# First edge layer of a two-layer graph network: a ring of 14 gathered tiles per stream, gathers issued tile by tile, one-hots turned one step ahead, a new order of the step

## The chip, the core and the metric

The kernel runs on one core of a Trainium2 chip. The metric is the device time of one execution in microseconds. The core has five engines that run on their own and wait for one another through counters: PE (TensorE, matrix products into PSUM), DVE (VectorE), ACT (ScalarE), POOL (GpSimd, which here issues the indirect loads) and SP (SyncE, which issues the other loads and stores). Each works through its own instructions in the order in which the program gives them.

## The reference, cut to what matters

A graph of N = 6250 nodes with E = 100000 edges, sorted by their destination `dst`; 512 features in 8 heads of 64. Two layers follow one another, each on a normalized input, with a residual. The first, which is changed, is attention over the edges that arrive at a node:

```python
h = leaky_relu(feat @ W.T + b, 0.2).reshape(N, 8, 64)
e_src, e_dst = (h * w_att_src).sum(-1), (h * w_att_dst).sum(-1)
e = leaky_relu(e_src[src] + e_dst[dst], 0.2)
m = segment_max(e, dst);  ex = exp(e - m[dst]);  s = segment_sum(ex, dst)
a = ex / s[dst] * dist
out = segment_sum(h[src] * a[:, :, None], dst)
```

The second layer takes the mean of `x[src]` over the edges of a node, two matrix products and a normalization.

## The kernel before, in words

**Stages.** A prologue normalizes x, multiplies it by the weights and writes `h0_d`: one row of 520 numbers per node, 512 of h and 8 of e_src. Its gathers for the first steps are issued at 242.5 us and after. Then comes the first edge layer (adds from 317.5 to 1575.3 us), a change-over, the second edge layer (adds from 1617.7 to 2802.9 us) and a short end.

**Tiling.** The sorted edges are cut into NQ = 4 streams. Each stream has 196 tiles of 128 edges, and a step k takes T = 3 tiles (j = 0, 1, 2) of each stream, so there are NW = 66 steps, the last of one tile. A gather (L717) is one indirect load of 128 rows of 2080 bytes for one stream and one tile: 12 a step. Its rows land in `gbuf`, which holds NB = 4 steps: 4 x 4 streams x 3 tiles x 520 numbers in each partition. The gathers of step k+4 are put into the program at the end of step k, stream by stream and in a stream tile by tile, into the slots of step k. A gather therefore waits for the adds (A..) of step k that read its slot.

**What a step does.** Streams go in two pairs, p = 0 and p = 1. The names are those of the table `STEPS`; the number ahead of a function there says for which later step the work is done in the pass of step k.

- OH (L760, DVE): one-hot matrices of the 128 edges of each tile against the 64 destination rows of the window. FT0, FT1 (L779, PE) turn them, for p = 0 and 1, in one PSUM bank ("t"); FT0c, FT1c (L783, ACT) copy the result to `oht`.
- FD (L791, PE): e_dst of each edge, as a product with `oht`, into the bank "z", once for each p. EC (L803, ACT) picks the e_src column out of the gathered rows into `es`; SS (L797, PE) adds it in "z", by three products, one per tile.
- EZ (L809, ACT) copies "z" to `e`. NX (L822, DVE) scans the first LA = 2 tiles of it backwards for the running maximum that the step before needs; SCF (L815) scans forwards; SCR (L829) joins both.
- TE, TM (L841, PE) turn `e` and the maxima back to one edge per partition; CM (L846, ACT) copies them; LM, SUB (DVE), EXP (ACT), AA (L871, L875, DVE) give the weights of the edges.
- D0a, D0b, D1a, D1b (L935, DVE), D0c (L942, DVE) and H01 to H13 (L954, ACT) multiply the gathered rows in place by the weights. Tiles 0 and 1 are DVE's, tile 2 is nearly all ACT's.
- A00 to A12 (L967, L970, PE; first digit p, second digit j) add the rows into the destination window by one-hot products; C0, C1 (L978, L979) carry over what the step before left open; EV0, EV1 (L988, L990, ACT) copy the sums out and SP stores them (L1001). CS makes the matrix for C0 and C1; SCR to F9b between the named ones handle rescaling in the first steps.
- S and L are single operations of the node work on finished rows ("slots": residual, normalization, store of `h1_d`). AT0, AT1 turn edge attributes every few steps.

**What sets the order.** The text `ORDER` is written out by hand and is run once for each k from -4 to 66. It fixes the order of the instructions on every engine. EC works for step k+2, so the gathers of step k+2 must have landed when ACT comes to EC in the pass of k.

**End of the layer.** The last LATES = 7 slots are worked after the layer. Their x rows are loaded by `late_x` into `keep`, seven loads on SP's queue in the passes 61 to 64 (L1119). An eighth place of `keep` belongs to the slot before them. Their sums are loaded after the layer (`sa`, L1168). In the last steps but one, IDLE, POOL takes part of the multiplications, since its gathers are all issued.

Of the kernel before, what the change touches and what calls it, by code (L numbers as in the profile page):

```python
# [8 lines left out]
FT = mybir.dt.float32  # L9
# [16 lines left out]
LA = 2  # L26
NB = 4
# [17 lines left out]
def gnn_kernel(ctx, tc, x, srcp, dstp, attrp, wt0, b0, wsrc, wdst, wts, wtn, bias1, gamma1, beta1, out):  # L45
# [648 lines left out]
    keep = kp.tile([128, LATES + 1, D], FT, name="keep")  # L694
# [3 lines left out]
    gbuf = gp.tile([128, NB, NQ, T, RW], FT, name="gbuf")  # L698
# [13 lines left out]
    def gather(k):  # L712
        GT[k] = g_ = gbuf[:, k % NB]
        for q in range(NQ):
            for j in range(njof(k)):
                c = k * T + j
                G.indirect_dma_start(out=g_[:, q, j, :], out_offset=None, in_=h0_d,  # L717
                                     in_offset=bass.IndirectOffsetOnAxis(ap=idx[:, q, c:c + 1], axis=0))
# [74 lines left out]
    def soft_src(k):  # L793

        z, es = ZP[k], ES_.pop(k)
        for j in range(njof(k)):
            P.matmul(z[0:NQ * H, j * 128:j * 128 + 128], es[:, j], ident, start=False, stop=True,  # L797
                     skip_group_check=True)

    def soft_pick(k):  # L800
        nj = njof(k)
        ES_[k] = es = lp.tile([128, T, NQ * H], FT, name="es")
        A.activation(es[:, 0:nj].rearrange("p j (q h) -> p j q h", q=NQ),  # L803
                     GT[k][:, :, 0:nj, D:RW].rearrange("p q j h -> p j q h"), AF.Copy)

    def soft_copy(k):
        n = njof(k) * 128
        E_[k] = e = lp.tile([NQ * H, T * 128], FT, name="e")
        A.activation(e[:, 0:n], ZP[k][0:NQ * H, 0:n], AF.Copy)  # L809
# [119 lines left out]
    def message(k, p, i):  # L929

        if i < njof(k) - (njof(k) == T and not (p and k in IDLE)):
            eng = G if p and i and k in IDLE else V
            q = slice(2 * p, 2 * p + 2)
            x4 = GT[k][:, q, i, 0:D].rearrange("p b (h d) -> p b h d", h=H)
            eng.tensor_tensor(out=x4, in0=x4, in1=(AA if eng is V else A2)[k][:, i, q].unsqueeze(3).to_broadcast([128, 2, H, D // H]),  # L935
                              op=OP.mult)

    def message_part(k):

        if njof(k) == T:  # L940
            x3 = GT[k][:, 0, T - 1, 0:D // 2].rearrange("p (h d) -> p h d", d=D // H)
            V.tensor_tensor(out=x3, in0=x3, in1=AA[k][:, T - 1, 0, 0:H // 2].unsqueeze(2).to_broadcast([128, H // 2, D // H]),  # L942
                            op=OP.mult)

    def message_act(k, p, i):

        if njof(k) == T and p and k in IDLE:
            if i == 0:
                message(k, p, T - 1)
        elif njof(k) == T:  # L950
            q2, h0 = divmod(4 * i, H)
            for h in range(h0, h0 + 4):
                x_ = GT[k][:, 2 * p + q2, T - 1, h * 64:h * 64 + 64]
                A.activation(x_, x_, AF.Copy, scale=A2[k][:, T - 1, 2 * p + q2, h:h + 1])  # L954

    def add_up(k, p, j):
# [8 lines left out]
        for q2 in range(2):  # L965
            r = slice(64 * q2, 64 * q2 + 64)
            P.matmul(w[r, :], oh[:, p, j, q2], g_[:, 2 * p + q2, j, 0:D], start=(j == 0), stop=False, skip_group_check=True)  # L967
# [52 lines left out]
    def slot_load(s, r=None):  # L1020
        if r is None:
            r = S.value_load(tab[0:1, s:s + 1], min_val=0, max_val=NP - 128)
        sa = lp.tile([128, AW], FT, name="sa0")
        S.dma_start(sa, acc0_d[ds(r, 128), :])
        sx = lp.tile([128, D], FT, name="sx", bufs=3) if s + 1 != LATE[0] else keep[:, LATES]
        S.dma_start(sx, x[ds(r, 128), :])
        SA[s] = (r, sa, sx)
# [61 lines left out]
    def slot(w):  # L1089
# [8 lines left out]
        FT0=(3, front_turn, 0), FT0c=(3, front_copy, 0), FT1=(2, front_turn, 1), FT1c=(2, front_copy, 1),  # L1098
        FD=(2, front_dst), EC=(2, soft_pick), SS=(2, soft_src), EZ=(2, soft_copy), SCF=(2, max_before), NX=(2, max_ahead),
# [8 lines left out]
        EV0=(0, evac0), EV1=(-1, evac1), OH=(3, onehot), CS=(0, later(carry_sel)))  # L1108
    STEPS.update({f"H{p}{i}": (0, message_act, p, i) for p in range(2) for i in range(4) if p or i})
    ORDER = """  # L1110
    H01 S CS H10 FT1 FT1c D0a S A00 D1a D0b H11 S FD TE EC SS H02 EV1 RESC EZ H03 D0c L S H12 NX S A01 AT0 SCR RS
    FL FDf FX RH S A10 OH A02 S S TM C0 CM AT0c FT0 AT1 D1b H13 EV0 S LM PF S SUB F9a F9b S A11 A12 SCF S C1 EXP AT1c AA S
    FT0c
    """.split()

    def late_x(i):

        ROW[LATE[i]] = r = S.value_load(tab[0:1, LATE[i]:LATE[i] + 1], min_val=0, max_val=NP - 128)
        S.dma_start(keep[:, i], x[ds(r, 128), :])  # L1119
# [43 lines left out]
    own1 = wp1.tile([128, LATES, D], FT, name="own1")  # L1163
    small = lay1.enter_context(tc.tile_pool(name="small1", bufs=5))
    with tc.tile_pool(name="tmp1", bufs=len(LATE)) as lp, tc.tile_pool(name="raw1", bufs=1) as tmp:
        for i, s_ in enumerate(LATE):
            sa = lp.tile([128, AW], FT, name="sa0")
            S.dma_start(sa, acc0_d[ds(ROW[s_], 128), :])  # L1168
            SA[s_] = (ROW[s_], sa, keep[:, i])
# [128 lines left out]
    def own_place(s):  # L1298
        n = s - LATE[0]
        return own1[:, n] if n >= 0 else keep[:, LATES] if n == -1 else attrs[:, (n + 3) * D:(n + 4) * D]  # L1300
# [421 lines left out]
```

## Time and profile before

| | |
|---|---|
| Median of 3 runs | 2924.06 us (2885.43 to 2945.61) |
| The profiled execution | 2861.34 us |
| its span, first to last instruction | 2859.5 us |
| PE, DVE, ACT, POOL busy | 76%, 55%, 39%, 60% of the span |
| 12 gathers a step, each | 967 ns on POOL |
| Bytes moved | 611.74 MB, 214 GB/s over the span |
| First edge layer, adds of step 0 to adds of step 62 | 317.5 to 1540.7 us |

The profile is of one execution. A row of a group of instructions reads: line of the kernel, engine, operation, what is written <- what is read, count | busy us, mean ns of one | idle us of the engine just before these instructions, and what ended most of that. A row of a timeline reads: start, duration, engine, line, what, and in brackets how long the engine had been idle and what ended it. In the waits, the numbers are us in total, times, and the longest. "remote" stands for a releaser that the profile can't name; "issue" for a time in which it shows nothing that the engine waited for. The ends of PE's rows are modelled.

### The profile page before, as it was taken

The page shows a single profiled execution, that of the slowest core. Times are in us where ns is not written, and L with a number is a line of the kernel's source. Part 1 is how long each engine was busy: PE and PEld are TensorE (multiplying, and loading weights), DVE is VectorE, ACT ScalarE, POOL GpSimd, SP SyncE. Part 2 cuts the span into 40 slices and gives each one's busy share as a digit, 9 for nine tenths or more (in the row PEclk, how much of TensorE's full clock was granted, in tenths as well). Part 3 has the DMA queues.
Part 4 walks back from the last instruction along what each step waited for, and adds up shares of the span by engine and source line. Part 5 has one row for each costly group of instructions (what it writes and reads, how often), then busy time and mean ns, then how long its engine had stood idle before and what let it go on. Part 6 is the DMA issues. An engine that isn't in the chain of part 4 may idle for free.

```text
span 2859.5 us, 35868 instructions
## 1 busy us (share of the span) xinstructions
PE 2174.2 (76%) x9688; PEld 1069.5 (37%) x9688; DVE 1583.2 (55%) x3363; ACT 1111.5 (39%) x3384; POOL 1706.5 (60%) x1679
## 2 busy tenths in 40 slices
PE   7993567777767878877878357787878879788876
PEld 5761233333333333333333123343433434343433
DVE  8875455564656656666666512254545445454556
ACT  5750344555555556555555301122222222222212
POOL 4565455655555656656663466666666666666662
PEclk9996688988888999889888678898989889898988
DMA  6535566777777777877776667778888777888862
GB/s 211 183 110 152 137 170 167 202 229 212 223 211 211 237 228 229 239 222 223 236 220 182 207 201 213 232 245 252 244 255 245 252 243 246 254 244 253 247 208 86
DMA packets 264719, 611.74 MB, mean 214 GB/s; under 512 B 63604, under 2 KB 74372, under 8 KB 264510
## 3 DMA queue, kind: packets, MB, share of 16 engines
q0 software_dynamic: 125440, 414.35, 50.1%
q1 hardware_dynamic: 138494, 193.97, 20.9%
q8 instruction: 80, 1.31, 0.2%
q14 instruction: 129, 1.06, 0.1%
q10 hardware_dynamic: 576, 1.05, 0.1%
HBM read 511.44 MB, written 97.76 MB: 213 GB/s over the span
## 4 chain that ended last, share of the span: by engine, by line
PE 39%; DVE 17%; issue 17%; another core or an unknown queue 13%; ACT 8%; DMA 3%; POOL 1%; SPq 1%; ACTq 0%; DVEq 0%; POOLq 0%
PE ps_w L967 9%; PE ps_w L1255 7%; PE ps_f L573 4%; PE ps_w L978 3%; PE ps_z L791 3%; PE ps_b L573 3%; ACT gbuf L954 3%; PE ps_w L1262 2%; PE ps_z L797 2%; DVE gbuf L935 1%; PE ps_t L779 1%; DVE clo L1277 1%; DVE hr L613 1%; PE ps_b L841 1%
## 5 line engine op out<-in xcount | busy, mean ns | idle before, releaser
L717 POOL DMA_INDIRECT gbuf<-h_d,idx x784 | 758.2, 967 | 546.3 <-issue 202.5
L1157 POOL DMA_INDIRECT g<-h_d,idx x784 | 771.5, 984 | 402.5 <-issue 227.0
L967 PE MATMUL ps_w<-gbuf,oh 128*64 128x512 f32 x1568 | 496.6, 674 | 66.8 <-issue 61.5
L1255 PE MATMUL ps_w<-g,oh 128*64 128x512 f32 x1568 | 440.7, 659 | 132.4 <-issue 65.3
L954 ACT ACTIVATE gbuf<-gbuf,aa 128x64 f32<-128x64 f32 x1788 | 461.9, 335 | 26.4 <-DVE aa L875 10.5
L935 DVE TENSOR_TENSOR gbuf<-gbuf,ps_c 128x1024 f32<-128x1024 f32 x260 | 304.9, 1199 | 0.0
L822 DVE TENSOR_TENSOR_SCAN nx<-penb,ms,ps_z 32x256 f32<-32x256 f32 x66 | 48.2, 730 | 456.9 <-issue 249.9
L791 PE MATMUL ps_z<-oht,edb 128*32 128x384 f32 (+1 forms) x264 | 129.1, 587 | 194.5 <-issue 118.0
L1265 ACT ACTIVATE ws<-ps_w 128x512 f32<-128x512 f32 x132 | 78.9, 598 | 450.5 <-remote 187.8
L1276 DVE CAST chi<-ws 128x512 fp32r<-128x512 f32 x130 | 68.2, 525 | 328.5 <-issue 244.3
L1255 PEld LDWEIGHTS ps_w<-g,oh 128*64 128x64 f32 x1568 | 99.0, 144 | 305.4 <-issue 262.3
L783 ACT ACTIVATE oht<-ps_t 128x384 f32<-128x384 f32 x132 | 63.7, 483 | 310.9 <-remote 231.0
L608 POOL TENSOR_TENSOR pr<-hr,watt 128x1024 f32<-128x1024 f32 x47 | 113.3, 2411 | 93.1 <-DVE hr L606 76.8
L967 PEld LDWEIGHTS ps_w<-gbuf,oh 128*64 128x64 f32 x1568 | 94.3, 149 | 148.3 <-issue 131.7
L978 PE MATMUL ps_w<-ws,cs 128*128 128x512 f32 x228 | 142.3, 709 | 0.0
L760 DVE TENSOR_TENSOR oh<-ps_c,dsr 128x768 f32<-128x768 f32 x130 | 121.3, 933 | 0.1
L970 PEld LDWEIGHTS ps_s<-ex,oh 128*64 128x64 f32 x792 | 66.3, 147 | 138.3 <-issue 137.6
L779 PE MATMUL ps_t<-ident,oh 128*128 128x128 f32 x392 | 76.0, 306 | 51.6 <-issue 26.1
L970 PEld LDWEIGHTS ps_f<-ex,oh 128*64 128x64 f32 x776 | 64.5, 147 | 131.8 <-issue 131.8
L791 PEld LDWEIGHTS ps_z<-oht,edb 128*32 128x32 f32 x264 | 21.2, 117 | 241.2 <-issue 149.0
L1323 ACT ACTIVATE hi<-ps_t 128x512 fp32r<-128x512 f32 x55 | 32.5, 591 | 186.4 <-remote 113.2
L809 ACT ACTIVATE e<-ps_z 32x384 f32<-32x384 f32 x66 | 31.4, 476 | 180.1 <-remote 62.4
(381 smaller groups left out, 4037.5 us busy)
## 6 DMA issues: line engine op xcount, KB each, us to landing
sx<-x SPq DMA_DIRECT2D x95, 256.0 KB
acc_d<-ws SPq DMA_DIRECT2D x182, 130.2 KB
acc_d<-ws SPq DMA_DIRECT2D x182, 128.0 KB
sa<-acc_d SPq DMA_DIRECT2D x55, 260.5 KB
h_d<-hr SPq DMA_DIRECT2D x49, 260.0 KB
gbuf<-h_d,idx POOLq DMA_INDIRECT x784
g<-h_d,idx POOLq DMA_INDIRECT x784
s<-acc_d SPq DMA_DIRECT2D x48, 256.0 KB
```

The source lines that it names most:

```text
L573: P.matmul(pt, a_[:, k], w_[:, k], start=not last[0], stop=stop and k == 3 and w_ is whi_ and a_ is lo)
L608: (G if t < NT - 2 else V).tensor_tensor(out=pr, in0=hr[:, None, 0:D].to_broadcast([128, 2, D]), in1=watt, op=OP.mult)
L717: G.indirect_dma_start(out=g_[:, q, j, :], out_offset=None, in_=h0_d, in_offset=bass.IndirectOffsetOnAxis(ap=idx[:, q, c:c + 1], axis=0))
L760: V.tensor_tensor(out=oh.rearrange("p a j b n -> p (a j b) n"), in0=c_iota[:, None, :].to_broadcast([128, 4 * T, M]), in1=dsr[:, k].rearra ...
L791: P.matmul(z[0:NQ * H, 0:n], ed_tile(k, p), oht[:, p, 0:n], start=(p == 0), stop=False, skip_group_check=True)
L935: eng.tensor_tensor(out=x4, in0=x4, in1=(AA if eng is V else A2)[k][:, i, q].unsqueeze(3).to_broadcast([128, 2, H, D // H]), op=OP.mult)
L954: A.activation(x_, x_, AF.Copy, scale=A2[k][:, T - 1, 2 * p + q2, h:h + 1])
L967: P.matmul(w[r, :], oh[:, p, j, q2], g_[:, 2 * p + q2, j, 0:D], start=(j == 0), stop=False, skip_group_check=True)
L970: P.matmul(sv[r, p], oh[:, p, j, q2], ex[:, j, 2 * p + q2], start=(j == 0 and p == 0), stop=False, skip_group_check=True)
L978: P.matmul(w, CS[k][:, p], c[:, p, 0:D], start=False, stop=True, skip_group_check=True)
L1157: G.indirect_dma_start(out=g_[:, q2, j, :], out_offset=None, in_=h1_d[0:NT * 128, :], in_offset=bass.IndirectOffsetOnAxis(ap=idx[:, 2 * p ...
L1255: P.matmul(BK[p][64 * q2:64 * q2 + 64, :], OHs[k][:, p, j, q2], GT[k, p][:, q2, j, :], start=(j == 0), stop=False, skip_group_check=True)
```

## The change

The ring holds NR = 14 tiles of each stream in place of 4 steps of 3: tile c of a stream lies in slot c modulo 14. The gathers of a step go tile by tile, and for each tile over the four streams. The space comes from `keep` (eight places of 2 KB in each partition become one, `kept`) and from `e` (one buffer in place of two); the seven x loads of the late slots are made after the layer, each behind the `sa` load of its slot, into a `keep` of the second layer's space. OH works for step k+4 (before k+3) and FT1 for k+3 (before k+2), so both halves of the turned one-hots are ready a whole step before FD. EC and SS are split: EC0 and SS0 take tiles 0 and 1, EC1 and SS1 tile 2, and EC copies each tile by its own instruction. The order of the step is new.

```diff
+NR = 14
...
-    keep = kp.tile([128, LATES + 1, D], FT, name="keep")
+    kept = kp.tile([128, D], FT, name="kept")
...
-    gbuf = gp.tile([128, NB, NQ, T, RW], FT, name="gbuf")
+    gbuf = gp.tile([128, NR, NQ, RW], FT, name="gbuf")
...
-        GT[k] = g_ = gbuf[:, k % NB]
-        for q in range(NQ):
-            for j in range(njof(k)):
+        GT[k] = [gbuf[:, (k * T + j) % NR] for j in range(njof(k))]
+        for j in range(njof(k)):
+            for q in range(NQ):
                 c = k * T + j
-                G.indirect_dma_start(out=g_[:, q, j, :], out_offset=None, in_=h0_d,
+                G.indirect_dma_start(out=GT[k][j][:, q, :], out_offset=None, in_=h0_d,
...
+    def part(k, i):
+
+        return range(min(LA, njof(k))) if i == 0 else range(LA, njof(k))
+
+    def soft_src(k, i):
+
+        z, es = ZP[k], ES_[k]
+        for j in part(k, i):
             P.matmul(z[0:NQ * H, j * 128:j * 128 + 128], es[:, j], ident, start=False, stop=True,
                      skip_group_check=True)
...
-        A.activation(es[:, 0:nj].rearrange("p j (q h) -> p j q h", q=NQ),
-                     GT[k][:, :, 0:nj, D:RW].rearrange("p q j h -> p j q h"), AF.Copy)
+    def soft_pick(k, i):
+        if i == 0:
+            ES_[k] = lp.tile([128, T, NQ * H], FT, name="es")
+            ES_.pop(k - 2, None)
+        for j in part(k, i):
+            A.activation(ES_[k][:, j].rearrange("p (q h) -> p q h", q=NQ), GT[k][j][:, :, D:RW], AF.Copy)
...
-        E_[k] = e = lp.tile([NQ * H, T * 128], FT, name="e")
+        E_[k] = e = lp.tile([NQ * H, T * 128], FT, name="e", bufs=1)
...
-        FT0=(3, front_turn, 0), FT0c=(3, front_copy, 0), FT1=(2, front_turn, 1), FT1c=(2, front_copy, 1),
-        FD=(2, front_dst), EC=(2, soft_pick), SS=(2, soft_src), EZ=(2, soft_copy), SCF=(2, max_before), NX=(2, max_ahead),
+        OH=(4, onehot), FT0=(3, front_turn, 0), FT0c=(3, front_copy, 0), FT1=(3, front_turn, 1), FT1c=(3, front_copy, 1),
+        FD=(2, front_dst), EC0=(2, soft_pick, 0), EC1=(2, soft_pick, 1), SS0=(2, soft_src, 0), SS1=(2, soft_src, 1),
+        EZ=(2, soft_copy), SCF=(2, max_before), NX=(2, max_ahead),
...
-    H01 S CS H10 FT1 FT1c D0a S A00 D1a D0b H11 S FD TE EC SS H02 EV1 RESC EZ H03 D0c L S H12 NX S A01 AT0 SCR RS
-    FL FDf FX RH S A10 OH A02 S S TM C0 CM AT0c FT0 AT1 D1b H13 EV0 S LM PF S SUB F9a F9b S A11 A12 SCF S C1 EXP AT1c AA S
-    FT0c
+    EC0 D0a FD SS0 H01 EV1 S A00 CS D0b L H02 TE S A01 RESC D0c H03 EC1 S FT0 SS1 D1a S NX FT0c H10 AT0 A02 S EZ C0 D1b
+    SCR RS FL FDf S FX RH EV0 TM AT0c A10 S H11 SCF CM OH FT1 LM PF S SUB H12 EXP A11 H13 AT1 F9a F9b S AA S A12 S FT1c C1 S
+    AT1c S
...
-        ROW[LATE[i]] = r = S.value_load(tab[0:1, LATE[i]:LATE[i] + 1], min_val=0, max_val=NP - 128)
-        S.dma_start(keep[:, i], x[ds(r, 128), :])
+        ROW[LATE[i]] = S.value_load(tab[0:1, LATE[i]:LATE[i] + 1], min_val=0, max_val=NP - 128)
...
+    keep = wp1.tile([128, LATES, D], FT, name="keep")
...
             S.dma_start(sa, acc0_d[ds(ROW[s_], 128), :])
+            S.dma_start(keep[:, i], x[ds(ROW[s_], 128), :])
```

## The prediction

> **What bounds the kernel now.** I read the summary page first, for the one group that idles most beside its own work: the gathers on POOL.
>
> ```profile
> span 2859.5 us, 35868 instructions
> ...
> L717 POOL DMA_INDIRECT gbuf<-h_d,idx x784 | 758.2, 967 | 546.3 <-issue 202.5
> ...
> L822 DVE TENSOR_TENSOR_SCAN nx<-penb,ms,ps_z 32x256 f32<-32x256 f32 x66 | 48.2, 730 | 456.9 <-issue 249.9
> ```
>
> A step has 12 gathers. One takes 967 ns, and 0.30 us pass between two that wait for nothing: 12 x 1.267 = 15.2 us. The idle time of 546.3 us less 784 x 0.30 = 235 leaves 311 us of true waiting, 4.7 us a step. Together 19.9 us. The trace's adds agree: the first add of step 0 starts at 317.5 and that of step 62 at 1540.7 us, so 62 steps take 1223 us, 19.7 us each. So POOL's two terms make the step. What it waits for is in its timeline:
>
> ```profile
> 905.49 0.94 POOL L717 DMA_INDIRECT gbuf<-h_d,idx  x1 [0.30 <-PE ps_f L732]
> 906.74 0.94 POOL L717 DMA_INDIRECT gbuf<-h_d,idx  x1 [0.30 <-issue]
> 907.98 0.94 POOL L717 DMA_INDIRECT gbuf<-h_d,idx  x1 [0.30 <-issue]
> 910.66 0.94 POOL L717 DMA_INDIRECT gbuf<-h_d,idx  x1 [1.73 <-PE ps_z L791]
> ...
> 915.65 0.94 POOL L717 DMA_INDIRECT gbuf<-h_d,idx  x1 [0.30 <-issue]
> 918.10 0.94 POOL L717 DMA_INDIRECT gbuf<-h_d,idx  x1 [1.51 <-remote]
> ```
>
> A pause after every six gathers: two streams by three tiles. The order is stream by stream, so the first six need PE's adds with p=0 of the step just done, the next six those with p=1. ACT at the same place:
>
> ```profile
> 910.58 0.49 ACT L783 ACTIVATE oht<-ps_t 128x384 f32<-128x384 f32 x1 [2.37 <-PE ps_z L791]
> ...
> 917.82 0.48 ACT L809 ACTIVATE e<-ps_z 32x384 f32<-32x384 f32 x1 [4.13 <-remote]
> ```
>
> ACT's two waits end within 0.3 us of POOL's. Both wait on PE's counter: the transposes (L779) that 910.58 waits for end in PE's rows at 907.95, and the sums (L797) that 917.82 waits for at 913.09. PE's news reaches the others 2 to 5 us after its rows. I can't name the cause; I take the lateness as given. The waits of 450 to 1450 us, about 50 steps, show who pays:
>
> ```profile
> DVE nx L822 <- issue: 222.7, 32, 10.5
> ACT oht L783 <- remote: 156.3, 26, 9.9
> ...
> DVE nx L822 <- ACT e L809: 133.9, 17, 10.6
> ```
>
> The scan ahead (nx) sits 357 us, 7 us a step, behind ACT's copy e; and the copy oht stands right before the matmul that needs it. Last, the stretches with and without gathers:
>
> ```profile
> 900.00:1000.00 100.00, 82.28 (x430) 37.49 (x429) 66.64 (x144) 58.54 (x215) 62.88 (x66) 0.91 0.79 234
> 1560.00:1570.00 10.00, 9.14 (x63) 4.47 (x61) 9.10 (x29) 5.55 (x21) 3.76 (x2) 1.00 0.66 189
> ```
>
> Columns: PE, its loads, DVE, ACT, POOL, granted clock, DMA share, GB/s. The last gather was issued at 1535.8. Step 62, the last with its full work on the usual engines, then takes 12.0 us (adds from 1540.7 to 1552.7). So arithmetic alone does not need 19.7 us; gathers and their handshake with PE do.
>
> **The skill.** "Perfetto Trace Analysis", Optimization Strategy (under Identifying Performance Opportunities): a gap that repeats on the engine that should be full can mean too few buffers for the next tile. The pause at every sixth gather agrees. "DMA: Bandwidth & Descriptors", Anatomy of one DMA — SWDGE (gpsimd) path: a wait is held on the issuing engine, not by the DMA engines, so a full slot stops every gather behind it; the POOL rows agree. "TensorE: Matmul & The Clock Gate", Architectural detail: ACT, DVE and GpSimd are strict first-in, first-out. The trace agrees: H03's scaling (918.21) follows the late e (917.82), and the second half of the add A02 starts only at 919.31.
>
> **The change, part by part**, per step, against the profiled execution (span 2859.5, 2861.3 with what lies around it; the median of the runs, 2924.1, is 2.2% higher, and I apply the same saving to it).
>
> *Ring of 14, tile by tile.* Gathers of step k+4 now fill slots that were read by tiles 1 and 2 of step k-1 and tile 0 of step k, not by all of step k. Eight of the twelve need nothing from step k, and the last four only its adds A00 and A10. They are needed at EC0 and EC1 of two steps later, so a slot is free 1.5 to 2 steps ahead instead of about 1.2. Same 12 instructions: 15.2 us stay; of the 4.7 us of waiting most can go. Bounds: 0 to 4.7 gained.
>
> *One-hots a step ahead.* The same 6 transposes, 2 copies and one compare a step, no new work. FD no longer stands behind the copy oht (about 3 us a step by the waits above: 156 us over 50 steps). The copy's late wait moves to the end of the step, with A11 and A12 (2 x 1.07 us of PE rows) between FT1 and its copy. If that cover fails, the late one is FD of the next step, as now.
>
> *New order.* NX now stands before EZ, so it waits for PE's first two sums (SS0), with CS, D0b, D0c and D1a between on DVE (0.41 + 1.20 + 0.41 + 1.20 = 3.2 us); EZ follows later and is used only in the next step. The 7 us of nx are not one more saving: they are the same step waiting in another engine. EC0 becomes the first thing on ACT: behind it stand H01 to H03, and behind these A00, A01 and A02. It waits for two tiles of gathers; the ring covers that.
>
> *EC split.* One copy of 0.27 us becomes three; the nearest ACT rows (128x18, 0.17; 128x1, 0.20) make that 3 x 0.19 = 0.57, so +0.3 us on an ACT that is busy 58% of the time: hidden; uncovered it would be 0.3 x 66 = 20 us. SS is three matmuls as before. One buffer for e: EZ must follow TE, with A01, FT0, SS1 and A02 (about 3.4 us of PE rows) between.
>
> *Late x loads.* Seven 256 KB loads leave steps 61 to 64 and follow the sa loads after the layer. SP needs 0.52 us for each (3.49 us for the seven sa): +3.6 us; by bytes 1.8 MB at the 350 GB/s of 1590 to 1600 us is 5 us. DVE paces that stretch (busy 9.6 of 10 us), hiding some. I take 5 us lost, bounds 0 and 9.
>
> *Sum.* Without POOL's pauses three loads are nearly equal: POOL 15.2 us; DMA, mean share 0.763 over 500 to 1500 us, x 19.7 = 15.0; PE, mean 77.6%, x 19.7 = 15.3. None runs at 100%. PE's best stretch in this layer is 91%: 15.3 / 0.91 = 16.8 us. So 19.7 - 16.8 = 2.9 us a step, x 62 = 180 us, less 5: 175. 2861 - 175 = 2686 profiled; 2924 - 175 = 2749 as a median. The second layer (1617 to 2803 us) is untouched.
>
> **Rivals.**
>
> *Floor.* PE's clock rises from about 0.88 to the 1.00 of 1560 us as its gaps close; PE's 15.3 falls to 13.5 and POOL's 15.2 bounds: 4.5 x 62 - 5 = 274, 2650. For it: the 12.0 us step. Against it: DMA at 15.0 would run at 99%, while its best 10 us here have 94%.
>
> *Lateness stays.* Ring and order remove one of the two pauses and the other keeps half of 4.7 us: 15.2 + 2.3 = 17.5; 2.2 x 62 - 5 = 131, 2793. For it: the second layer, with a ring of 2.5 steps and its own order, also takes about 18 us a step. Against it: in the new order nearly every PE product has 2 to 4 us before its reader.
>
> *Slower.* PE's news seems to come about 1.4 us after POOL pauses, at both places above. If POOL must pause for it, a longer ring makes POOL run longer first, and SS0's and TM's news, which follow each other in a step, both wait for a pause. Now a step is 2 x (6 gathers, 7.6, + 1.5 pause + 0.75) = 19.7. With the 0.75 at 1.5 us it is 21.2, so 1.5 x 62 + 5 = 98 lost, 3022. It decides once the two extras together exceed today's 1.5 us. Against it: the transposes of L841 (TE, TM) reach ACT within 1 us of their rows in 42 of the 45 waits for them, with POOL running.
>
> *Hidden anyway.* Gathers that land no later than now are read no sooner; then only the order counts, which is the third case's time.
>
> **Chances.** Forecast 2749: 0.47. Lateness stays 2793 (its own spread 2740 to 2890): 0.23, of which 0.05 within 2% of now. Floor 2650: 0.16. Slower 3022: 0.14, of which 0.03 within 2%. A measurement of this kernel tells about 2% (2866 to 2983) from no change: faster 0.79, within 0.08, slower 0.13. The range of 8 in 10 leaves out the slower case and ends of the others: 2640 to 2890.
>
> **What would show it.** Right: the idle of the L717 row down from 546 to some 360 us; POOL's pauses no longer at every sixth gather; PE at 88 to 92 of 100 us in mid-layer with a clock above 0.91; nx waiting under 2 us a step; the layer's last adds at about 1395 instead of 1575; 1617 to 2803 only shifted. Wrong: gathers back to back while ACT still waits 3 us or more at L783 or e, or ACT's first copy EC0 waiting for gathers; then the step stays above 18 us. A stretch between the last add and the first gather of the second layer longer by over 9 us would make my price of the late loads wrong.

## The result, and the profile after

The changed kernel took 2972.9 us (median of four runs, 2963.7 to 2976.1) beside 2929.7 us for the kernel before: ratio 1.034, interval 1.028 to 1.040. It is slower, and the forecast of 2749 us was wrong. The profiled execution took 2976.1 us; its span is 114.8 us longer than that of before (2974.3 against 2859.5). That is much more than the 43 us between the medians, since the profiled execution of before, 2861.3 us, was quicker than all four of its timed ones (2885.4 and more). Read from the adds in the two traces, the 114.8 us are:

| Stretch | Before | After | Difference |
|---|---|---|---|
| Start of the span to the first add of step 0 | 317.5 | 328.2 | +10.7 |
| 62 steps of the first layer | 1223.2 (19.73 each) | 1334.4 (21.52 each) | +111.2 |
| Steps 62 to 65, to the end of the last add | 34.6 | 42.3 | +7.7 |
| Last add to first add of the second layer | 42.4 | 44.2 | +1.8 |
| Second layer and end | 1241.8 | 1225.2 | -16.6 |

So the loss is in the steady steps. The summary page of the changed kernel, for the two groups that the prediction shows of before:

```profile
span 2974.3 us, 36284 instructions
...
PEclk9995688778777777788887967889899898989997
...
L718 POOL DMA_INDIRECT gbuf<-h_d,idx x784 | 749.0, 955 | 669.0 <-PE ps_w L973 346.0
...
L828 DVE TENSOR_TENSOR_SCAN nx<-penb,ms,ps_z 32x256 f32<-32x256 f32 x66 | 48.2, 730 | 572.2 <-remote 269.6
```

The gathers are as quick as before (955 ns), but POOL idles 669 us ahead of them instead of 546. Less 784 x 0.30 that is 434 us of waiting, 6.6 us a step against 4.7. The sum of the prediction closes again: 12 x 1.255 + 6.6 = 21.7, the trace has 21.5. The scan nx idles 572 us instead of 457. The timeline of one step, the one with the longest of these waits, shows how (start, duration, engine, line, what, idle before and what ended it):

```profile
1009.77 0.95 POOL L718 DMA_INDIRECT gbuf<-h_d,idx  x1 [5.28 <-PE ps_w L973]
...
1012.85 0.94 POOL L718 DMA_INDIRECT gbuf<-h_d,idx  x1 [2.13 <-PE ps_f L976]
...
1014.09 0.95 POOL L718 DMA_INDIRECT gbuf<-h_d,idx  x1 [0.30 <-DVE gbuf L948]
...
1018.74 0.55 PE L780 MATMUL ps_t<-ident,oh 128*128 128x128 f32 x3
...
1024.13 0.95 POOL L718 DMA_INDIRECT gbuf<-h_d,idx  x1 [0.30 <-issue]
1025.38 0.95 POOL L718 DMA_INDIRECT gbuf<-h_d,idx  x1 [0.30 <-issue]
...
1028.81 0.49 ACT L784 ACTIVATE oht<-ps_t 128x384 f32<-128x384 f32 x1 [11.00 <-remote]
...
1028.85 0.73 DVE L828 TENSOR_TENSOR_SCAN nx<-penb,ms,ps_z 32x256 f32<-32x256 f32 x1 [13.63 <-remote]
...
1031.68 0.52 PE L847 MATMUL ps_b<-ident,mr 32*128 32x32 f32 x3 [9.81 <-DVE mr L835]
...
1034.38 1.08 POOL L718 DMA_INDIRECT gbuf<-h_d,idx  x1 [8.05 <-PE ps_w L973]
```

From 1012.85 POOL issues eleven gathers in a row. PE turns the one-hots (L780) at 1018.74, by its own row in under a microsecond. ACT, which needs nothing else for its copy, starts at 1028.81: 2.5 us after POOL's last gather ended (1026.33). The scan nx starts in the same moment. Only then come the scan for mr, PE's turning of mr (TM), the weights, the adds, and with them POOL's next gather, after 8.05 us. Every engine waits in turn for one late piece of news, that is for PE's count as the others see it. The waits of 450 to 1450 us (us in total, times, longest) say that such waits, mostly shorter ones, are the rule:

```profile
POOL gbuf L718 <- PE ps_w L973: 263.1, 63, 8.0
DVE nx L828 <- remote: 156.4, 16, 13.6
DVE nx L828 <- PE ps_w L973: 142.4, 17, 10.4
ACT oht L784 <- remote: 139.5, 25, 11.0
```

I counted POOL's runs in the traces between 450 and 1400 us: a run ends where the next gather starts over 2 us after the one before. The kernel before has mostly runs of 5 to 7 (70 of them), with 12 of 10 or 11 and 27 single gathers between two stops; the pause after every six gathers, which the prediction read from one stretch, is not its only pattern. The changed kernel has 42 runs of 2 and 42 of 10 or 11, nearly without exception in turn. They break at the 9th gather of a step (stopped for 2.3 us on the average) and at the 11th (5.0 us).

### The profile page after: what moved, and what is told of

Same layout as the page of the kernel before. It is cut to its first block, busy times and chain, and to the rows that moved or that the text cites. A ratio compares the mean times of both kernels' runs of the same rounds, so it can differ in the third digit from the quotient of the medians.

```text
span 2974.3 us, 36284 instructions
## 1 busy us (share of the span) xinstructions
PE 2253.0 (76%) x9688; PEld 1123.4 (38%) x9688; DVE 1612.8 (54%) x3363; ACT 1132.9 (38%) x3514; POOL 1697.0 (57%) x1679
## 3 DMA queue, kind: packets, MB, share of 16 engines
q1 hardware_dynamic: 138494, 193.97, 19.9%
## 4 chain that ended last, share of the span: by engine, by line
PE 34%; DVE 20%; issue 19%; another core or an unknown queue 13%; ACT 5%; POOL 4%; DMA 3%; SPq 1%; DVEq 0%; ACTq 0%; POOLq 0%
PE ps_w L973 9%; PE ps_w L1263 6%; PE ps_f L574 3%; POOL gbuf L718 3%; DVE gbuf L941 3%; PE ps_b L574 2%; PE ps_w L984 2%; PE ps_z L792 2%; PE ps_w L1270 2%; DVE mr L835 1%; DVE oh L761 1%; DMA gbuf<-h_d,idx 1%; DVE clo L1285 1%; PE ps_t L780 1%
## 5 line engine op out<-in xcount | busy, mean ns | idle before, releaser
L718 POOL DMA_INDIRECT gbuf<-h_d,idx x784 | 749.0, 955 | 669.0 <-PE ps_w L973 346.0
L973 PE MATMUL ps_w<-gbuf,oh 128*64 128x512 f32 x1568 | 572.7, 766 | 32.8 <-issue 29.7
L941 DVE TENSOR_TENSOR gbuf<-gbuf,ps_c 128x1024 f32<-128x1024 f32 x260 | 313.4, 1206 | 0.0
L1273 ACT ACTIVATE ws<-ps_w 128x512 f32<-128x512 f32 x132 | 78.8, 597 | 463.3 <-remote 142.4
L994 ACT ACTIVATE ws<-ps_w 128x512 f32<-128x512 f32 x132 | 78.7, 596 | 283.9 <-PE ps_w L973 76.8
L984 PE MATMUL ps_w<-ws,cs 128*128 128x512 f32 x228 | 156.0, 770 | 3.6 <-issue 3.6
L847 PE MATMUL ps_b<-ident,mr 32*128 32x32 f32 x196 | 30.8, 273 | 156.0 <-DVE mr L835 156.0
L973 PEld LDWEIGHTS ps_w<-gbuf,oh 128*64 128x64 f32 x1568 | 102.2, 161 | 107.3 <-issue 91.2
L802 PE MATMUL ps_z<-ident,es 128*32 128x128 f32 x392 | 69.6, 288 | 92.9 <-issue 53.0
L780 PE MATMUL ps_t<-ident,oh 128*128 128x128 f32 x392 | 90.6, 349 | 40.3 <-issue 39.2
L574 PE MATMUL ps_f<-ws_whi,hi 128*128 128x512 f32 x112 | 55.3, 494 | 75.0 <-issue 48.6
```

Of the source, the lines that this page charges most:

```text
L574: P.matmul(pt, a_[:, k], w_[:, k], start=not last[0], stop=stop and k == 3 and w_ is whi_ and a_ is lo)
L718: G.indirect_dma_start(out=GT[k][j][:, q, :], out_offset=None, in_=h0_d, in_offset=bass.IndirectOffsetOnAxis(ap=idx[:, q, c:c + 1], axis=0))
L780: P.transpose(pt[:, j * 128:j * 128 + 128], OHs[k][:, p, j].rearrange("e b n -> e (b n)"), ident)
L973: P.matmul(w[r, :], oh[:, p, j, q2], g_[j][:, 2 * p + q2, 0:D], start=(j == 0), stop=False, skip_group_check=True)
L984: P.matmul(w, CS[k][:, p], c[:, p, 0:D], start=False, stop=True, skip_group_check=True)
```

## The experiments

Two theories stood at first. **P**: PE's counter reaches the others only some 1.5 to 2.5 us after POOL stops issuing gathers, and the change makes POOL's runs longer. **O**: the new order itself is longer (without gathers its steps take 14 us, those of before 11 to 12). A third, **T**: the bytes of the gathers delay the counter, not their issue.

**First four: each part alone, rests, half the bytes.**

`ring_only` keeps ring, tile-by-tile gathers, split EC and late loads, and goes back to the order and lookahead of before:

```diff
-    EC0 D0a FD SS0 H01 EV1 S A00 CS D0b L H02 TE S A01 RESC D0c H03 EC1 S FT0 SS1 D1a S NX FT0c H10 AT0 A02 S EZ C0 D1b
...
+    H01 S CS H10 FT1 FT1c D0a S A00 D1a D0b H11 S FD TE EC0 EC1 SS0 SS1 H02 EV1 RESC EZ H03 D0c L S H12 NX S A01 AT0 SCR RS
...
```

> The changed kernel with the order and the lookahead of the one-hots of before: only the ring of 14, the gathers tile by tile, the split EC and the late x loads are left. Theory P (pause): PE's counter reaches ACT and DVE only 1.5 to 2.5 us after POOL stops issuing gathers, and the longer ring lets POOL issue 8 to 12 in a row instead of 6. Then the ring alone loses: step 20.5 to 22 us against 19.7, ratio to before 1.02 to 1.05, runs of 8 and more gathers, waits of ACT or DVE of 6 to 10 us. Theory O (order): the new order itself is what costs (its steps without gathers take 14 us against 12), the ring is harmless: step 17.5 to 19.7, ratio 0.95 to 1.005.

`order_only` is the kernel before with the new `ORDER` and `STEPS` and the split EC and SS; ring, gather order, the two buffers for e and the late loads stay as before.

> The kernel before with the new order, the one-hots a step ahead and the split EC and SS; the ring stays at four steps, the gathers go stream by stream and the late x loads stay where they were. Theory P: POOL still stops after every six gathers, so the news is not later than before: step 19.0 to 20.3 us, ratio to before 0.98 to 1.015. Theory O: the order carries the loss: step 21.0 to 21.6, ratio 1.025 to 1.04.

`pause6` is the changed kernel with

```diff
+                if k >= NB - 1 and (j * NQ + q) % 6 == 5:
+                    for _ in range(8):
+                        G.memset(rest, 0.0)
```

> The changed kernel with a rest of 8 small memsets (together an estimated 2 to 3 us, from the rows of 122 ns for 32 and 555 ns for 528 columns) put on POOL behind every sixth gather, so that POOL never issues more than six in a row although the ring would let it. Theory P: more work on POOL, yet faster than the changed kernel, since the news comes in each rest: step 19.5 to 20.7 us, 2860 to 2930 us against 2973, nx and oht waits of 450 to 1450 us down by half or more. Theory O, or theory T (the DMA traffic as such delays the counter): nothing is gained, 2970 or above; with the rests uncovered up to 2 x 2.5 x 66 = 330 us slower.

`half_bytes` gathers half rows; the other half of each place stays zero:

```diff
-                G.indirect_dma_start(out=GT[k][j][:, q, :], out_offset=None, in_=h0_d,
+                G.indirect_dma_start(out=GT[k][j][:, q, RW // 2:RW], out_offset=None, in_=h0_d.rearrange("n (a w) -> (n a) w", a=2),
```

> The changed kernel with gathers of 128 x 1040 bytes instead of 2080: only the second half of each place in the ring is loaded (from a half row), the first half stays zero; so the messages are not the reference's. Number and issue of the gathers are as in the changed kernel, bytes are halved. Theory P: the lateness stays: runs of 8 to 12 gathers, waits of 8 to 13 us at nx and oht, step above 20 us. Theory T (traffic): the waits shrink to under 3 us and the step falls to 15.5 to 17.5 us.

Measured: on this chip the kernel before itself took 2385.5 us. `ring_only` 2384.4 (ratio 0.999, 0.998 to 1.000), `order_only` 2387.5 (1.000, 0.999 to 1.001), `half_bytes` 2387.9, `pause6` 2675.4. None of the theories had foreseen that: there was no lateness to act on. Between 450 and 1400 us POOL issued some 620 gathers in one run without a stop, and the three variants without rests took 15.3 to 15.5 us a step, which is POOL's own 12 x 1.27. `pause6` took 19.9 us, which is 15.2 + 2 x 2.3: POOL's work and nothing else. What the first four do show is that the late news isn't a property of the kernel alone.

**The two kernels again.** Both as they are, to see which of this holds on the next chip.

> The changed kernel as it is, beside the kernel before, on the chip that this call gets. In the first four experiments the kernel before itself ran at 2385 us instead of 2925, at 15.3 us a step in both layers, and with no late counter. Theory C (the lateness of PE's counter belongs to the chip or the hour and not to the kernel): if the kernel before runs near 2385 here, the two kernels agree within 0.5% (both at POOL's 12 x 1.27 us a step); if it runs near 2925, the changed kernel is 2.5 to 4% slower. Theory K (the change brings a loss of its own): 1.5% or more slower also beside a kernel before of 2385 us, because the steps without gathers and the late loads cost more.

> The kernel before as it is, to have its profile beside the changed kernel's on the same chip. Theory C: on an undisturbed chip POOL issues its gathers every 1.25 us nearly without a pause, step 15.2 to 15.5 us, and ACT and DVE wait for PE by its rows, without lateness. Theory K: it still pauses after every six gathers for 1 us or more.

This chip was of the other kind: the kernel before took 2877.9 us, the changed one 2968.9, ratio 1.039 (1.026 to 1.052). `before_again` had 20.5 us a step, the changed kernel 21.5, so that in this pair of profiles the loss is 1.0 us a step and not 1.8. The rows, of before and of the changed kernel:

```profile
L717 POOL DMA_INDIRECT gbuf<-h_d,idx x784 | 766.2, 977 | 583.6 <-issue 189.2
```

```profile
L718 POOL DMA_INDIRECT gbuf<-h_d,idx x784 | 748.0, 954 | 664.5 <-PE ps_w L973 329.5
```

Less 235 us each that is 5.3 us of waiting a step against 6.5. In the kernel before POOL still stopped between its runs, now 41 of 5 to 7 gathers, 25 of 10 or 11 and 46 single ones. So runs of ten occur there as well, though its gathers go stream by stream.

**The first four once more**, on another chip.

> The same kernel as ring_only, hoped for on a chip on which PE's counter is late (the kernel before at 2840 to 2950 us there; on a chip without lateness it is 2385 and nothing new is learnt). Theory P: the ring alone makes POOL's runs longer and the news later: step 21 to 22 us, ratio to before 1.015 to 1.05. Theory O (the new order suffers from lateness, the ring does not): step 19 to 20.5, ratio 0.97 to 1.005.

> The same kernel as order_only, hoped for on a chip with late counters. Theory P: POOL still stops after every six gathers: step 19 to 20.6, ratio 0.97 to 1.01. Theory O: step 21 to 22, ratio 1.02 to 1.045.

> The same kernel as pause6 (the changed kernel with a rest of 2.3 us on POOL after every sixth gather), hoped for on a chip with late counters. On a chip without lateness its step was 19.9 us, which is POOL's 15.2 + 2 x 2.3. Theory P: the rests let the news through, so that the lateness costs nearly nothing more: step 19.9 to 20.7 us, 2850 to 2920 us, faster than the changed kernel (2970) although POOL has 4.6 us more to do in a step. Theory O or T: rests do not help, step 21.5 us or more, 2970 us or more.

> The same kernel as half_bytes (only half of each gathered row is loaded, the rest stays zero), hoped for on a chip with late counters. Theory P (issue of gathers delays the news): step above 20.5 us, SP's register operations of 0.7 us and waits of 8 us and more at nx and oht stay. Theory T (bytes delay the news): step 15.3 to 17.5 us, no waits above 4 us.

It had no late counters again (kernel before 2388.6 us): 2386.6, 2391.2, 2680.7 and 2390.1 us, nothing new. From here on I call the two kinds of chips late and prompt. Late are three chips of these experiments, with the kernel before at 2836 to 2946 us, and, by its profile, the chip of the result; prompt are three others, with 2377 to 2396 us. Only one chip was met twice, prompt both times; that the kind belongs to the chip and not to the hour is likely but not shown.

**One kernel with several treatments.** Since the chip couldn't be chosen, `mix1` compares treatments inside one run; `after_3` is the changed kernel beside it.

```diff
+                half, none_ = 46 <= k < 57, 57 <= k < 65
+                if none_:
+                    continue
...
+                every, n = (6, 8) if 24 <= k < 35 else (3, 4) if 35 <= k < 46 else (0, 0)
+                if every and (j * NQ + q) % every == every - 1:
+                    for _ in range(n):
+                        G.memset(rest, 0.0)
```

> The changed kernel as it is, once more, to have it beside the kernel before on whichever chip this call gets. Theory C (the loss needs a chip with late counters): beside a kernel before of 2385 us it takes 2380 to 2400 us, ratio 0.995 to 1.005; beside one of 2840 to 2950 us the ratio is 1.02 to 1.05. Theory K (a loss of its own): ratio above 1.015 also beside 2385 us.

> The changed kernel with stretches of its gathers handled differently, so that one run compares them: gathers of steps 3 to 23 as they are; 24 to 34 with a rest of 2.3 us on POOL behind every sixth; 35 to 45 with a rest of half that behind every third; 46 to 56 with half of each row loaded (1040 bytes; the other half of the place keeps old numbers); 57 to 64 without any gather (old numbers are used). So its output is not the reference's. On a chip with late counters, theory P (issue of gathers delays the news): steps of 21 to 22.5 us as they are, 19.9 to 20.7 with rests behind six, 20 to 22 with the short rests, above 20.5 with half the bytes, 12 to 14.5 without gathers, where SP's slow operations vanish. Theory T (bytes): half the bytes 15.5 to 18 us. On a chip without: 15.3, 19.9, 19.9, 15.3, 14 to 15.

The chip was late: the kernel before 2886.3 us, `after_3` 3010.6, ratio 1.051 (1.039 to 1.062). `mix1`, by POOL's gathers:

| Gathers of steps | Treatment | us a step |
|---|---|---|
| 8 to 23 | as they are | 21.8 |
| 24 to 34 | rest of 2.3 us behind every sixth | 20.0 |
| 35 to 45 | rest of half that behind every third | 20.6 |
| 46 to 56 | half the bytes | 21.0 |
| 57 to 64 | no gathers (by the adds of steps 55 to 61) | 14.5 |

With the long rests the timeline of POOL, and of the copy oht and the scan nx, is this:

```profile
859.60 2.27 POOL L728 MEMSET rest<- 128x160 f32 x8
...
861.35 0.49 ACT L793 ACTIVATE oht<-ps_t 128x384 f32<-128x384 f32 x1 [4.68 <-PE ps_w L993]
861.39 0.73 DVE L837 TENSOR_TENSOR_SCAN nx<-penb,ms,ps_z 32x256 f32<-32x256 f32 x1 [8.16 <-PE ps_w L993]
862.34 0.95 POOL L723 DMA_INDIRECT gbuf<-h_d,idx  x1 [0.47 <-issue]
863.60 1.33 POOL L723 DMA_INDIRECT gbuf<-h_d,idx  x1 [0.31 <-issue]
...
869.00 0.95 POOL L723 DMA_INDIRECT gbuf<-h_d,idx  x1 [0.31 <-issue]
869.95 2.27 POOL L728 MEMSET rest<- 128x160 f32 x8
872.37 0.95 POOL L723 DMA_INDIRECT gbuf<-h_d,idx  x1 [0.16 <-issue]
```

Its own rests apart, POOL waits no more than 0.5 us ahead of a gather, but for one wait of 3.1 in the eleven steps. It has 4.6 us more work in a step and is still 1.8 us quicker, at the 20.0 us that its work adds up to; on a prompt chip the same rests gave the same 19.9. The copy oht (861.35) and the scan nx (861.39) start inside the rest (859.60 to 861.87): they still wait, but the news comes through there, ahead of the stop that it would else cause. So P holds. With half the bytes the pattern of the changed kernel comes back:

```profile
1293.95 0.95 POOL L723 DMA_INDIRECT gbuf<-h_d,idx  x1 [4.73 <-PE ps_w L982]
1295.20 0.94 POOL L723 DMA_INDIRECT gbuf<-h_d,idx  x1 [0.30 <-issue]
...
1305.23 0.95 POOL L723 DMA_INDIRECT gbuf<-h_d,idx  x1 [0.30 <-issue]
1308.74 0.95 POOL L723 DMA_INDIRECT gbuf<-h_d,idx  x1 [2.56 <-PE ps_s L742]
1309.99 0.95 POOL L723 DMA_INDIRECT gbuf<-h_d,idx  x1 [0.31 <-issue]
1315.25 0.94 POOL L723 DMA_INDIRECT gbuf<-h_d,idx  x1 [4.31 <-PE ps_w L982]
```

The window of this stretch and of the one without gathers (PE, its loads, DVE, ACT, POOL, granted clock, DMA share, GB/s):

```profile
1280.00:1430.00 150.00, 114.86 (x532) 52.98 (x532) 83.47 (x173) 78.01 (x293) 75.35 (x80) 0.77 0.44 124
1465.00:1560.00 95.00, 87.72 (x522) 43.26 (x519) 78.98 (x164) 71.78 (x273) 3.79 (x4) 1.00 0.31 87
```

At a DMA share of 0.44 and 124 GB/s the stops of 2.6 and 4.3 to 4.7 us are all there, so T falls: halving the bytes doesn't help. A half row leaves the 128 rows and the issue of a gather as they are, and its packets fall only from 80 to 48, so what of a gather delays the news, its issue or its rows on the queues, isn't separated. Without gathers PE is busy 92% at full clock on this late chip, and the copies oht that had to wait start 0.04 us after their product (0.1 once in eight): so the lateness is gone there, and the lower clock of the other steps (0.77 with half the bytes) comes and goes with the gathers and isn't a lasting mark of the chip.

**Which part makes the runs of ten.** `ring_only_3` and `order_only_3` are `ring_only` and `order_only` again. `mix2` is the changed kernel with other rests, and with a ring of 12 at the end:

```diff
-        GT[k] = [gbuf[:, (k * T + j) % NR] for j in range(njof(k))]
+        GT[k] = [gbuf[:, (k * T + j) % NR if k < 51 else ((k - 51) * T + j) % 12] for j in range(njof(k))]
...
+                every, n = (6, 5) if 18 <= k < 29 else (12, 8) if 29 <= k < 40 else (6, 3) if 40 <= k < 51 else (0, 0)
```

> The same kernel as ring_only, for the third time in the hope of a chip with late counters (the kernel before near 2890 us; beside 2385 us nothing new is learnt). Theory P, part ring: the longer ring lets POOL run longer: step 21 to 22 us, ratio to before 1.015 to 1.05. Theory O (order): step 19 to 20.8, ratio 0.97 to 1.005.

> The same kernel as order_only, for the third time in the hope of a chip with late counters. Theory P, part ring: POOL still stops after every six gathers: step 19 to 20.8, ratio 0.97 to 1.01. Theory O: step 21 to 22, ratio 1.02 to 1.05.

> The changed kernel with other rests by stretches of gathers: steps 3 to 17 as they are; 18 to 28 a rest of 1.4 us (five memsets) behind every sixth gather; 29 to 39 one of 2.3 us behind every twelfth; 40 to 50 one of 0.85 us behind every sixth; 51 and after no rest, but a ring of 12 tiles in place of 14. Nothing is left out. On a chip with late counters, theory P: POOL's time a step 21.5 to 22 us, then 18.0 to 19.5 (15.2 + 2.8 and little lateness), 19 to 21, 20 to 22; with the ring of 12, if the ring's length is what lets POOL run on, 19.5 to 20.7, and as without rest (21.5 to 22.3) if it is not. On a chip without: 15.3, 18.1, 17.6, 17.0, 15.3.

The chip was late (kernel before 2909.0 us). `ring_only_3`: 2871.5 us, ratio 0.987 (0.981 to 0.993), 19.8 us a step, against the "21 to 22" that P had for it. `order_only_3`: 2777.7 us, ratio 0.955 (0.949 to 0.961), 18.6 us a step, better than either theory had. So O falls: the order is no burden, it is the gain. `order_only_3` is clearly faster than the kernel before and `ring_only_3` slightly (1.3%); both together are slower than it: the changed kernel was not timed whole on this chip, but its first stretch in `mix2` took 21.4 us a step here. The rows and the waits of the two:

```profile
L718 POOL DMA_INDIRECT gbuf<-h_d,idx x784 | 759.8, 969 | 553.3 <-issue 176.4
```

```profile
L717 POOL DMA_INDIRECT gbuf<-h_d,idx x784 | 774.9, 988 | 460.7 <-issue 175.4
```

The first is `ring_only_3`, the second `order_only_3`: 553 and 461 us of idle against 669 for both together (the profile of the result). The runs agree. Counted as above, `ring_only_3` has 43 runs of 4 and 42 of 8; `order_only_3` has 102 of 5 to 7 and none longer. A piece of its timeline:

```profile
904.13 0.94 POOL L717 DMA_INDIRECT gbuf<-h_d,idx  x1 [0.30 <-issue]
...
906.79 0.49 ACT L783 ACTIVATE oht<-ps_t 128x384 f32<-128x384 f32 x1 [5.76 <-remote]
...
906.84 0.73 DVE L827 TENSOR_TENSOR_SCAN nx<-penb,ms,ps_z 32x256 f32<-32x256 f32 x1 [6.33 <-remote]
...
907.59 0.94 POOL L717 DMA_INDIRECT gbuf<-h_d,idx  x1 [2.51 <-ACT oht L783]
...
923.63 0.95 POOL L717 DMA_INDIRECT gbuf<-h_d,idx  x1 [0.30 <-PE ps_t L779]
...
926.37 0.49 ACT L783 ACTIVATE oht<-ps_t 128x384 f32<-128x384 f32 x1 [4.70 <-PE ps_w L983]
...
926.41 0.73 DVE L827 TENSOR_TENSOR_SCAN nx<-penb,ms,ps_z 32x256 f32<-32x256 f32 x1 [8.02 <-PE ps_w L983]
```

The lateness is there as well: ACT and DVE start together, 1.7 and 1.8 us after the end of POOL's last gather (905.07 and 924.58). But the stops come earlier: between 450 and 1450 us ACT's longest wait at this copy is 5.8 us, and 11.0 in the changed kernel.

`mix2`, by POOL's gathers: as they are 21.4 us a step; rest of 1.4 us behind every sixth 19.5; rest of 2.3 behind every twelfth 23.9; rest of 0.85 behind every sixth 22.8; ring of 12 without rests 22.2. The two last rests are misses of the expectation, and tell something: 0.85 us is too short for the news to come (POOL still stops 6.7 us at the 11th gather), and a rest behind the twelfth lies two gathers behind the stop at the 11th, where nothing is due, and leaves the next ten in a row (stop of 6.8 us). The ring of 12 with tile-by-tile gathers, once the four steps that pass over to it are done, keeps the bad pattern, only four gathers later, at the first and third gather of the step (2.3 and 5.1 us; 21.9 us a step from step 55 on):

```profile
1458.47 0.95 POOL L719 DMA_INDIRECT gbuf<-h_d,idx  x1 [2.42 <-remote]
1459.72 0.94 POOL L719 DMA_INDIRECT gbuf<-h_d,idx  x1 [0.31 <-issue]
1465.92 0.94 POOL L719 DMA_INDIRECT gbuf<-h_d,idx  x1 [5.26 <-PE ps_w L978]
1467.17 0.95 POOL L719 DMA_INDIRECT gbuf<-h_d,idx  x1 [0.30 <-issue]
...
1477.18 0.95 POOL L719 DMA_INDIRECT gbuf<-h_d,idx  x1 [0.30 <-issue]
1480.45 0.94 POOL L719 DMA_INDIRECT gbuf<-h_d,idx  x1 [2.33 <-PE ps_w L978]
```

So the length of the ring is not what makes the run of ten. What remains between this stretch (22.2) and `order_only_3` (18.6, same chip, ring of 12, same order of the step) is the order of the gathers, with the layout of the ring that goes with it, and the single buffer for e; and ACT waits ahead of its copy into that buffer in the changed kernel only 2.0 us in 1000.

**The gathers stream by stream in the ring of 14.** `streams14` swaps the two loops of `gather` back and leaves all else as changed; `after_4` stood beside it.

```diff
-        for j in range(njof(k)):
-            for q in range(NQ):
+        for q in range(NQ):
+            for j in range(njof(k)):
```

> The changed kernel with its gathers issued stream by stream as before, and nothing else undone: ring of 14, new order, one buffer e, late loads after the layer. On chips with late counters (the kernel before near 2890 us) the mid-layer gathers came in runs of 10 and 2 in the changed kernel (21.5 to 21.9 us a step), of 8 and 4 with ring and gather order alone (19.8), of 6 with the new order alone (18.6). Theory G (the tile-by-tile order of the gathers makes the runs of 10): runs of at most 7, step 18 to 19.4 us, ratio to before 0.945 to 0.98. Theory R (the slack of the ring of 14 makes the long runs whatever their order): runs of 10 and more, step 21 us or more, ratio 1.02 to 1.05. Beside a kernel before of 2385 us: ratio 0.995 to 1.005 in both.

> The changed kernel as it is, beside streams14 on the same chip. Theory C: where the kernel before takes near 2385 us, ratio 0.995 to 1.005; where it takes near 2890 us, 1.02 to 1.05. Theory K: above 1.015 on either.

> The same kernel as streams14 (the changed kernel, gathers stream by stream), in the hope of a chip with late counters; the first time it met one without, where it is 1.0025 of before and nothing was learnt. In the changed kernel POOL stops at the 9th gather of a step (tile 2, which needs A00) for 2.3 to 2.5 us and at the 11th (needs A10) for 5.1, so ten go in a row between. Stream by stream the same two needs fall on the 3rd and the 9th. Theory G (order of the gathers): runs of 6, stops at the 3rd and 9th, step 18 to 19.4 us, ratio to before 0.945 to 0.98. Theory R (slack of the ring of 14): runs of 10 and more, step 21 us or more, ratio 1.02 to 1.05.

Both times the chip was prompt. `streams14` took 2391.7 us (1.0025, 1.0013 to 1.0037) and 2388.3 (1.0005, 0.999 to 1.002), and `after_4`, the changed kernel, 2389.0: ratio 1.0011, 0.9999 to 1.0023. So whether stream by stream in the long ring mends the loss on a late chip wasn't seen. What was seen is the changed kernel on a prompt chip: no loss. Its page, waits (450 to 1240 us) and a window:

```profile
span 2382.7 us, 36284 instructions
...
L718 POOL DMA_INDIRECT gbuf<-h_d,idx x784 | 757.1, 966 | 248.8 <-issue 139.6
...
L828 DVE TENSOR_TENSOR_SCAN nx<-penb,ms,ps_z 32x256 f32<-32x256 f32 x66 | 48.2, 730 | 170.7 <-PE ps_z L802 169.2
```

```profile
POOL gbuf L718 <- issue: 104.2, 342, 0.3
...
ACT oht L784 <- PE ps_t L780: 29.2, 26, 2.3
```

```profile
900.00:1000.00 100.00, 87.22 (x505) 41.37 (x504) 80.36 (x167) 72.13 (x273) 75.91 (x80) 1.00 0.92 289
```

POOL's idle time is the 0.30 us between two gathers and no more (784 x 0.30 = 235 of 248.8). The step is 15.26 us, and the copy oht never waits more than 2.3 us.

The best version on a late chip is `order_only`, at 0.955 of the kernel before; on the prompt ones it is level with it (1.0004 and 1.0014).

## Why the prediction was wrong

**The step that failed** is the first part of the sum: "of the 4.7 us of waiting most can go. Bounds: 0 to 4.7 gained." It measured 1.9 us lost (6.6 against 4.7), and 1.2 in the second pair of profiles. I had taken the lateness "as given", as if it would stay the same whatever POOL did, and took POOL's stops for waits for slots that PE had not yet read, which more slack ends; the reading of the repeated pause as too few buffers was the wrong one here. But the rows that I had quoted showed PE done 2 to 5 us before its news; and on a prompt chip `order_only`, with the short ring, has the same 248.9 us of idle ahead of its gathers as the changed kernel (248.8). The stops were when the news came. Slots that are free earlier let POOL run on, and the longer it runs, the more of PE's news has to wait for its stop. The lower bound of this term should have been below zero, because my own slower rival said so.

**"Eight of the twelve need nothing from step k, and the last four only its adds A00 and A10"** was right as a statement of the program, and is just what goes wrong. In the tile-by-tile order these four stand together: the 9th and 10th gathers need A00, the 11th and 12th A10, with POOL's stops at the 9th and 11th. From the 11th gather to the 8th of the next step POOL has ten gathers that wait for nothing. Stream by stream with four steps of slots, the needs are spread (first six gathers p = 0, last six p = 1), and in the new order, where A00 to A02 stand ahead of A10 to A12, they come half a step apart: runs of six. In the old order the same tile-by-tile gathers break into 4 and 8. Run length and step go together on late chips: up to 7 gathers, 18.6 us; 8 and 4, 19.8; the kernel before with its mixture, 19.7 and 20.5; 10 and 2, 21.5 to 21.9. That the gather order makes the runs of ten rests on `mix2` against `order_only_3`, and only together with the order of the step: the kernel before goes stream by stream and has 12 and 25 runs of 10 or 11 in its two traces. The direct test, stream by stream in the long ring, met no late chip, so this part is argued and not shown.

**The new order**: I had expected that "nearly every PE product has 2 to 4 us before its reader". The gain is there, if POOL is stopped often enough: `order_only_3` gains 131 us, 4.5%. It costs in the steps without gathers, which the sum left out: from the start of step 62 to the last add it takes 42.4 us, as the changed kernel does, and `ring_only_3` 34.5, as before. That FT a step ahead covers FD didn't help in the changed kernel, since a copy that begins up to 9.5 us after its product outlasts the cover.

**The late loads** cost 1.8 us where I took 5 (bounds 0 to 9): mis-sized, within its bounds. The split EC never showed: the waits of PE's weight loads for es are 4.9 us in 1000 in the changed kernel's trace. The second layer was only shifted, as said (18.0 us a step, 18.2 before). The start was not priced at all and cost 10.7 us (14 in the second pair of traces). The record puts it with the ring and its gathers: on one chip the first add starts at 326.1 us in `ring_only_3` and at 319.2 in `order_only_3`; why is open. The chances of the cases add up to 0.81 faster and 0.11 slower where the prediction writes 0.79 and 0.13; nothing rests on it.

**The rivals.** *Slower*, at 0.14, was what happened: it gave 21.2 us a step and 3022 us, measured are 21.5 and 2973. Between the medians it forecast 98 us lost, and 43 were. Its mechanism, news that comes after POOL stops, is shown by the rests; the place that it named, the longer ring, is not: in `mix2` the ring of 12 kept the runs of ten. Against it I had set that TE and TM reach ACT within 1 us in 42 of 45 cases. That evidence was misleading: it did not show how late the others are, nor when in POOL's run those 42 fall. In the same trace, between 450 and 1450 us, 48 of the 52 products TM ended while POOL was at a stop or no further than the third gather after one (stops of over 1 us counted), where 46 of them reached ACT within 1 us. Of the 62 products of FT0 and FT1 for which ACT had to wait, 44 ended later in a run than that, and all 44 reached it over 0.5 us late. *Floor* (15.2 us a step) is true of every version without rests that was profiled on a prompt chip (15.2 to 15.5), and by its time of the kernel before. *Lateness stays* had the sign wrong. My own signs of failure, "gathers back to back while ACT still waits 3 us or more at L783", describe the profile after well.

**What stays open**: why the news is late, and why on some chips only. Shown is that it needs gathers being issued, that half their bytes don't help, and that a rest of 2.3 us (or 1.4) behind every sixth lets it through while 0.85 does not. Nor is it shown whether PE's count leaves late or the waiting engines notice it late; that SP's own register moves are slowed too, as shown below, speaks for something wider than PE's count. Fetches of instructions are no sufficient reason: in the changed kernel's trace 24 of ACT's 36 waits of over 3 us at the copy oht have no packet of instructions in them.

## What to carry to other kernels

When an engine waits for a slot, look whether the reader of that slot had long been done; if so, more buffers need not help, and the thing to ask is what keeps the news. Where an engine's runs delay the others, the order of its instructions matters as much as the depth of its buffer: spread the needs that stop it evenly over the step. And try two changes apart before trying them together: here each gained alone on a late chip, and together they lost.

## What the hardware showed that I had not expected

- The kernel before takes 2377 to 2396 us on some chips and 2836 to 2946 on others. In the changed kernel's traces a step of the first layer takes 15.3 us or 21.5 to 21.9, one of the second layer 15.4 or 18.0 to 18.2.
- On late chips SP is slowed as well. In the trace's records between 500 and 1200 us, 8 to 14% of SP's register moves take over 0.5 us, typically 0.7, where the median is 29 ns; on the prompt chips not one does. In the step shown first, many of SP's small instructions take 0.7 us from 1020.9 to 1028.7, and PE's news comes as they turn quick.
- On late chips, in the kernel before and in both halves of the change, ACT's waits of over 3 us end at a median of 1.5 to 1.9 us after the last gather's end. In the changed kernel it is 3.0 us after the end of a run of ten, when POOL has already issued the next gather.
- How far POOL has got in its run when PE's product ends decides whether the news is late. On one late chip, between 450 and 1400 us, of the copies oht that had to wait: in `ring_only_3` 40 products ended by the second or third gather of a run, and 32 of them reached ACT within 0.5 us (median 0.04); in `order_only_3` 69 ended by the fourth or later, and none did (medians 2.2 to 4.0 us). On a prompt chip all 24 of the changed kernel came at a median of 0.04 us, in the middle of one unbroken run.
